# Where layer 1 of the second-to-last batches stands at the end of a two-layer graph network kernel

## The chip, the cores and the metric

The kernel runs on one core of a Trainium2 chip. A core has TensorE (PE, matmuls), VectorE (DVE), ScalarE (ACT), GpSimd (POOL) and SyncE (SP), and 16 DMA engines. Each engine works through its own queue of instructions in order; a wait in a queue holds up all that stands behind it. SP, ACT and POOL also issue DMAs. The metric is the device time of one execution in microseconds, the median over several runs.

## The reference

The input x has 32 batches of 512 rows with 512 features, and there is one adjacency matrix of 512 by 512. Per batch:

```
h = relu(layernorm(x));  x = x + (adj @ h) @ W0 + b0                 # layer 0
h = relu(layernorm(x));  x = x + attention(h; adj, Wq, Wk, Wv) @ Wo + bo   # layer 1
```

In layer 1 the mask is (1 - adj) * -1e9, so each row attends to the column where its adjacency entry is largest. Where that peak is clear enough, attention is a selection of one row: row n of the result is row idx[n] of h, times Wv times Wo. The kernel tests for this at the start and then takes `single_path`, the one profiled here. Only some of the 512 rows are ever selected (at most 336 here), so layer 1 need only be computed for those and then be handed out to all rows.

## The kernel before

A batch x is held in SBUF as four chunks of 128 rows, and five such buffers rotate (`xs`). For batch b there are three products on TensorE. `aggregate(b)` makes yT from h and adj, `layer0(b)` adds yT times W0 onto x, `layer1(b)` multiplies the selected rows of h with the product of Wv and Wo (`wvo`, kept from the start). Each product is a Strassen-like scheme of seven pieces (L364); a piece is a burst of matmuls into a PSUM bank, and its result is taken by VectorE or ScalarE (`take`, L401 and L403, L411 and L414, L421). The second piece on the same bank can't start before the first has been taken.

Around layer 1 stands a way through DRAM. `put_h` (L503) writes the rows of h by an indirect DMA into the order in which they are used, `get_h` (L515) reads the used rows back, `transpose_h` (L552) transposes them on VectorE, `hT_sum` forms the sums which the seven-piece scheme needs. After `layer1`, `put_z` (L570, L575) transposes the result z and writes it to DRAM in two parts (columns of rows 0 to 6 and 6 to S, in blocks of 32). `finish` (L579) gathers z for all rows with an indirect DMA that adds onto x in SBUF, and `store` (L598) writes x to the output.

The order is written out by hand: there is no scheduler. The loop at L620 goes over b from 0 to 32 and fills 21 lists of small jobs, `todo`, by `put(batch, step, job)`. Then it emits up to three products and, between each piece and its `take`, the jobs of one step: steps 0 to 6 go with `layer0(b)`, 7 to 13 with `aggregate(b + 1)`, 14 to 20 with `layer1(b - 1)`. Where there is no product, its jobs are simply emitted in order. So regularly TensorE does: layer 0 of b, aggregate of b + 1, layer 1 of b - 1.

The end differs. The last batch, 31, takes another way through layer 1: its h is stored plainly by SP (L500), gathered for all 512 rows (`get_all`, L522, on POOL), transposed by TensorE four blocks at a time (`transpose_all`, L529, with a copy by ACT, L530), and multiplied with `wvo` row block by row block (`layer1_rows`, L541 to L544). This way has a long latency: after the last piece of layer 0 there are the norm (L284 to L294), the relu (L302), the store, the gather, the transposes. To fill TensorE meanwhile, the kernel before holds back layer 1 of batch 29 as well as that of batch 30: TensorE does aggregate(31), layer0(31), layer1(29), layer1(30), the rows of 31. For batch 29 nothing is computed in its regular place in iteration 30 (`b != B - 2`), and layer1(29) stands at steps 7 to 13 of iteration 31, layer1(30) at steps 14 to 20.

As two batches are then late together, batch 30 needs buffers of its own: its transposed h goes into `adjT` and `adjT_s`, which are no longer used, its z into the tile h0s, the transposed z into the tile hc. And both batches get their z not by an accumulating gather but by `fetch` (L588), a plain gather into `sel` and `yT`, and by `add_z` (L593) on VectorE with an output DMA (L594) of its own. The adds stand in `layer1_rows`, two behind each row block of batch 31: those of batch 29 behind rows 0 and 1, those of batch 30 behind rows 2 and 3.

Of the kernel before, what the change touches and what calls it, by code (L numbers as in the profile page):

```python
# [8 lines left out]
F32 = mybir.dt.float32  # L9
# [8 lines left out]
P = 128  # L18
# [288 lines left out]
def single_path(ctx: ExitStack, tc: tile.TileContext, x, wv, bv, wo, bo, out, kept, room):  # L307
# [15 lines left out]
    nc = tc.nc  # L323
# [157 lines left out]
    def aggregate(b):  # L481
        return product(H0[b], H0S[b], adjT, adjT_s, take_new(yT))
# [52 lines left out]
    def layer1_rows(b):  # L535
        for r in range(C):
            bank = ps_m.tile([P, D], F32, name="mm")
            for d in range(DC):
                if d == 2 and r + 1 < C:
                    transpose_all(r + 1)  # L540
                nc.tensor.matmul(bank, hs[1][:, d, r * P:(r + 1) * P], wvo[:, d, :], start=(d == 0), stop=(d == DC - 1))  # L541
# [12 lines left out]

    def hT_sum(b, i):
        if i == 0:
            HTS[b] = adjT_s[:, :, :, 0:WIDE] if b == B - 2 else work.tile([P, 4, 2, WIDE], F32, name="hTs")
        sum_b(nc, HTS[b], HT[b], i, WIDE)

    def layer1(b):  # L560
        ZT[b] = work.tile([P, DC, 32 * S], F32, name="h0s" if b == B - 2 else "zs")
        if room < 32 * S:
            nc.gpsimd.memset(ZT[b][:, :, room:32 * S], 0.0)
        return product(wvo, wvo_t, HT[b], HTS[b], take_z(ZT[b]), WIDE)

    def put_z(b, s0, s1):
        if b not in Z:
            Z[b] = dram.tile([32 * S, D], F32, name="z")
            ZR[b] = work.tile([P, S, P], F32, name="hc" if b == B - 2 else "zr")
        nc.vector.transpose(ZR[b][:, s0:s1, :].rearrange("p s (c e) -> p s c e", c=4),  # L570
                            ZT[b][:, :, 32 * s0:32 * s1].rearrange("p c (s j) -> p s c j", j=32))
        rows = Z[b].rearrange("(s j) (q f) -> q j s f", j=32, q=4)
        for q in range(4):
            eng = nc.scalar if q > 1 and (b, s0) in ((B - 3, 6), (B - 2, 0)) else nc.sync
            eng.dma_start(rows[q][:, s0:s1, :], ZR[b][32 * q:32 * q + 32, s0:s1, :])  # L575

    def finish(b):
# [3 lines left out]
                in_offset=bass.IndirectOffsetOnAxis(ap=place[:, c:c + 1], axis=0), compute_op=ALU.add)  # L581


    late_z = {B - 3: sel, B - 2: yT}

    def fetch(b):
        for c in range(C):
            nc.gpsimd.indirect_dma_start(  # L588
                out=late_z[b][:, c, :], out_offset=None, in_=Z[b],
                in_offset=bass.IndirectOffsetOnAxis(ap=place[:, c:c + 1], axis=0))  # L590

    def add_z(b, c, eng):
        nc.vector.tensor_add(X[b][:, c, :], late_z[b][:, c, :], X[b][:, c, :])  # L593
        eng.dma_start(out[b, c * P:(c + 1) * P, :], X[b][:, c, :])  # L594

    def store(b):
# [20 lines left out]
    with tc.manual_schedule():  # L617
        nc.gpsimd.affine_select(out=upper, in_=ones, compare_op=ALU.is_ge, fill=0.0, base=-1,
                                pattern=[[1, P]], channel_multiplier=-1)
        for b in range(B + 1):  # L620
            todo = [[] for _ in range(21)]

            def put(batch, step, f, *args):
                if 0 <= batch < B:
                    todo[step].append(lambda: f(batch, *args))

            put(b - 2, 15 if b == B - 1 else 1, fetch if b > B - 2 else finish)
            if b < 2:
# [10 lines left out]
            for c, step in enumerate((1, 3, 9, 12) if b == 0 else (9, 10, 11, 12) if b == B - 2 else (14, 15, 17, 19)):  # L639
# [28 lines left out]
            for i, step in enumerate((13, 13, 13, 14) if b in (0, B - 2) else (14, 15, 16, 18)):  # L668
                put(b + 1, step, yT_sum, i)
            if b < B and b != B - 2:  # L670
                put(b - 1, 20, put_z, 6, S)
            ahead = []
            put(b + 2, 8, lambda b: ahead.append(ln0(b)))
            for c, step in enumerate((9, 10, 13, 13) if b > 0 else (8, 9, 10, 11)):
                put(b + 2, step, lambda b, c: ahead[0].stats(c), c)
            put(b + 2, 14 if b > 0 else 11, lambda b: ahead[0].power())
            put(b + 2, 17 if b > 0 else 12, lambda b: ahead[0].offset())
            for c, step in enumerate((17, 18, 19, 20) if b > 0 else (12, 13, 14, 14)):
                put(b + 2, step, lambda b, c: ahead[0].relu(c), c)
            if b == 0:  # L680
                put(0, 1, lambda b: number_rows())
                for i in (2, 3):
                    put(0, 12, lambda b, i: sum_b(nc, w0_t, w0_s, i), i)
                todo[3] += todo[4] + todo[5] + todo[6]
                run(layer0_rows(0), todo[0:4])
            if b == B - 1:
                put(b, 18, lambda b: transpose_all(0))
            if b == 1:
                tables = []
                put(1, 0, lambda b: tables.append(places()))  # L690
                put(1, 16, lambda b: look_up(tables[0]))
                for i, step in enumerate((5, 5, 6, 6)):
# [270 lines left out]
```

## Time and profile before

| | us |
|---|---|
| median of 3 runs | 1085.42 (1084.32 to 1086.23) |
| profiled execution, its own time | 1083.45 |
| its span (first to last instruction) | 1081.3 |
| PE busy | 1064.6 (98%) |
| DVE busy | 902.7 (83%) |
| POOL busy | 441.9 (41%) |
| ACT busy | 362.1 (33%) |

The profile is of one execution. Its span stands 2.1 us below the time of that execution, which takes in what lies around the instructions. In a timeline, each row has the start and the length in us, the engine, the line, the operation, its output and inputs by the program's names, and in brackets how long the engine had stood idle before and who released it. In the windows by time, the columns are the stretch, its length, the busy time of PE, of its weight loads, of DVE, ACT and POOL (with the number of instructions), the granted clock of TensorE as a share of full speed, the busy share of the DMA engines, and GB/s.

### The profile page before, as it was taken

The numbers are of one execution on the slowest core, as the hardware profiler recorded it, in microseconds if no ns is written. First come the engines' busy times: TensorE is split into PE (matmuls) and PEld (weight loads), VectorE is DVE, ScalarE is ACT, GpSimd is POOL, SyncE is SP. The second block draws the span as 40 slices with busy tenths as digits, with TensorE's granted clock in tenths as the row PEclk, the third lists the DMA queues.
The fourth block names the chain that finished last, engine by engine and source line by source line (L and its number), as shares of the span: only waits on it lengthen the run. The fifth ranks groups of instructions, "written<-read, shape, count | busy, mean of one in ns | idle before, by whom it ended". The sixth has DMA issues, their size and how long they took to land.

```text
span 1081.3 us, 15886 instructions
## 1 busy us (share of the span) xinstructions
PE 1064.6 (98%) x5404; PEld 939.3 (87%) x5404; DVE 902.7 (83%) x1850; ACT 362.1 (33%) x664; POOL 441.9 (41%) x522
## 2 busy tenths in 40 slices
PE   8999999999999999999999999999999999999996
PEld 4488998999998899988998998999998999999883
DVE  6789888888888788988888888888888888888874
ACT  6223422324432323432323432323432333442221
POOL 2024554343454343454433454433355434345513
PEclk9999999999999999999999999999999999999999
DMA  9144767666776566767656776666767666776537
GB/s 330 40 88 150 188 178 170 162 164 188 197 193 179 128 171 182 202 167 200 143 149 188 200 190 179 146 165 174 202 183 183 159 154 175 194 186 168 134 103 263
DMA packets 162443, 186.90 MB, mean 173 GB/s; under 512 B 15024, under 2 KB 102320, under 8 KB 162352
## 3 DMA queue, kind: packets, MB, share of 16 engines
q1 hardware_dynamic: 132464, 116.73, 36.4%
q0 software_dynamic: 27968, 66.61, 27.4%
q10 hardware_dynamic: 1920, 2.46, 0.7%
q8 instruction: 44, 0.72, 0.3%
q14 instruction: 47, 0.39, 0.1%
HBM read 96.28 MB, written 89.46 MB: 172 GB/s over the span
## 4 chain that ended last, share of the span: by engine, by line
PE 92%; DVE 3%; DMA 1%; POOL 1%; issue 1%; ACT 1%; SPq 0%; ACTq 0%; DVEq 0%; POOLq 0%
PE mm L364 87%; PE mm L134 1%; PE mm L206 1%; PE mm L491 1%; PE mm L541 1%; DVE st L284 1%; DMA yT<-z,place 1%; POOL x L579 1%; PE pt L106 0%; DVE x L421 0%; DMA x<-in_L_gnn_Wv_dram 0%; DVE x L471 0%; DMA hc<-hs 0%; ACT h L302 0%; DMA z<-zr 0%
## 5 line engine op out<-in xcount | busy, mean ns | idle before, releaser
L579 POOL DMA_INDIRECT x<-z,place x116 | 182.8, 1576 | 352.5 <-issue 196.7
L403 ACT COPY yT<-mm 128x512 f32<-128x512 f32 x124 | 71.9, 580 | 541.7 <-PE mm L364 482.7
L421 DVE TENSOR_TENSOR x<-mm,x 128x512 f32<-128x512 f32 x217 | 149.6, 690 | 85.7 <-PE mm L364 85.7
L302 ACT ACTIVATE h<-x,off,rstd 128x512 f32<-128x512 f32 x256 | 194.7, 807 | 54.2 <-DVE off L294 53.4
L291 POOL TENSOR_TENSOR rstd<-ve,mhalf 128x2 f32<-128x2 f32 (+1 forms) x97 | 106.7, 1100 | 229.6 <-DVE ve L290 229.0
L284 DVE BATCH_NORM_STATS2 st<-x 128x6 f32<-128x512 f32 x256 | 171.5, 670 | 2.6 <-DMA x<-in_x_dram 1.4
L364 PE MATMUL mm<-adjT_s,h0s 128*128 128x256 f32 x744 | 171.0, 379 | 0.3 <-ACT yT L403 0.3
L364 PE MATMUL mm<-w_t,sel 128*128 128x256 f32 x744 | 170.7, 379 | 0.0
L364 PEld LDWEIGHTS mm<-adjT_s,h0s 128*128 128x128 f32 x744 | 141.1, 190 | 20.4 <-ACT yT L403 1.3
L364 PEld LDWEIGHTS mm<-w_t,sel 128*128 128x128 f32 x744 | 141.3, 190 | 19.3
L503 POOL DMA_INDIRECT hs<-h,dest x124 | 128.6, 1037 | 23.8 <-issue 22.4
L364 PE MATMUL mm<-w_s,yT 128*128 128x256 f32 x496 | 117.2, 379 | 0.0
L364 PE MATMUL mm<-adjT,h 128*128 128x256 f32 x496 | 117.2, 379 | 0.0
L364 PE MATMUL mm<-hTs,wvo_t 128*128 128x168 f32 x720 | 112.5, 306 | 0.8 <-ACT zs L414 0.8
L414 ACT ACTIVATE zs<-mm,cvo_c 128x168 f32<-128x168 f32 x240 | 83.1, 398 | 77.3 <-PE mm L364 73.4
L364 PEld LDWEIGHTS mm<-hTs,wvo_t 128*128 128x128 f32 x720 | 105.4, 190 | 1.0 <-ACT zs L414 1.0
L364 PEld LDWEIGHTS mm<-adjT,h 128*128 128x128 f32 x496 | 94.2, 190 | 13.2 <-issue 0.5
L364 PEld LDWEIGHTS mm<-w_s,yT 128*128 128x128 f32 x496 | 92.9, 190 | 11.3
L471 DVE TENSOR_TENSOR x<-x,b_r 128x512 f32<-128x512 f32 x124 | 83.8, 676 | 0.0
L364 PE MATMUL mm<-hT,wvo 128*128 128x168 f32 x480 | 78.2, 306 | 0.0
L364 PEld LDWEIGHTS mm<-hT,wvo 128*128 128x128 f32 x480 | 72.7, 190 | 1.6
L401 DVE TENSOR_TENSOR yT<-mm,yT 128x512 f32<-128x512 f32 x93 | 64.0, 688 | 5.5 <-PE mm L364 1.5
(156 smaller groups left out, 1277.3 us busy)
## 6 DMA issues: line engine op xcount, KB each, us to landing
out_dram<-x SPq DMA_DIRECT2D x124, 256.0 KB
x<-in_x_dram SPq DMA_DIRECT2D x120, 256.0 KB
hc<-hs SPq DMA_DIRECT2D x124, 176.0 KB
z<-zr SPq DMA_DIRECT2D x120, 96.0 KB
z<-zr SPq DMA_DIRECT2D x118, 80.0 KB
hs<-h,dest POOLq DMA_INDIRECT x124
x<-z,place POOLq DMA_INDIRECT x116
adj_s<-in_adj_dram SPq DMA_DIRECT2D x2, 512.0 KB
```

The costliest lines, as they stand in the source:

```text
L134: nc.tensor.matmul(ps, wvT[:, j, i * P:(i + 1) * P], wo_s[:, j, :], start=(j == 0), stop=(j == DC - 1))
L284: self.nc.vector.bn_stats(st, self.src[:, self.chunks[i], :])
L291: self.nc.gpsimd.tensor_tensor(self.rstd, ve, self.mhalf[:, 0:n], ALU.pow)
L302: self.nc.scalar.activation(dst, src, AF.Relu, bias=self.off[:, i:i + 1], scale=self.rstd[:, i:i + 1])
L364: nc.tensor.matmul(bank[:, m, 0:half], lhs[:, k, m * P:(m + 1) * P], rhs[:, k, :], start=(first and m == 0 and k == 0), stop=(k == 1), ski ...
L401: nc.vector.tensor_add(dst, bank, dst)
L403: nc.scalar.copy(dst, bank)
L414: nc.scalar.activation(dst[:, m, :], bank[:, m, :], AF.Identity, bias=cvo_c[:, 2 * i + m:2 * i + m + 1])
L421: nc.vector.tensor_add(dst, bank, dst)
L471: nc.vector.tensor_add(X[b][:, c, :], X[b][:, c, :], b0_r)
L503: stored = nc.gpsimd.indirect_dma_start(out=HS[b], out_offset=bass.IndirectOffsetOnAxis(ap=dest[:, i:i + 1], axis=0), in_=H1[b][:, i, :], ...
L579: nc.gpsimd.indirect_dma_start(out=X[b][:, c, :], out_offset=None, in_=Z[b], in_offset=bass.IndirectOffsetOnAxis(ap=place[:, c:c + 1], axi ...
```

## The change

Layer 1 of batch 29 goes back to steps 14 to 20 of iteration 30. In iteration 31, steps 7 to 13 hold layer1(30), and steps 14 to 20 have no product; their jobs follow one another. TensorE then does aggregate(31), layer1(29), layer0(31), layer1(30), the rows of 31.

With it: batch 29 is finished by the accumulating gather (`finish`, at step 1 of iteration 31) and written by `store` (SP, at step 12 of iteration 31, behind the two stores of h at steps 9 and 11). Batch 30 alone is fetched late, into `yT`, and its four adds stand behind rows 2 and 3. The borrowed buffers of batch 30 are dropped. The transposes of batch 30's h move from steps 10 to 12 of iteration 31 to its steps 1 to 3, its sums from steps 12 to 14 to steps 4 and 5; z of batch 30 is put at step 13 of iteration 31 and at the start of the last iteration. In iteration 30, the sums of yT and the adds of b0 have their regular steps again.

```diff
-            for i in range(2):
-                add_z(B - 3 + r // 2, 2 * (r % 2) + i, nc.sync if r < 2 else nc.scalar)
+            if r > 1:
+                for i in range(2):
+                    add_z(B - 2, 2 * (r - 2) + i, nc.scalar)
...
-            HT[b] = adjT[:, :, 0:32 * S] if b == B - 2 else work.tile([P, DC, 32 * S], F32, name="hT")
+            HT[b] = work.tile([P, DC, 32 * S], F32, name="hT")
...
-        ZT[b] = work.tile([P, DC, 32 * S], F32, name="h0s" if b == B - 2 else "zs")
+        ZT[b] = work.tile([P, DC, 32 * S], F32, name="zs")
...
-            eng = nc.scalar if q > 1 and (b, s0) in ((B - 3, 6), (B - 2, 0)) else nc.sync
+            eng = nc.scalar if q > 1 and (b, s0) == (B - 2, 0) else nc.sync
...
-            put(b - 2, 15 if b == B - 1 else 1, fetch if b > B - 2 else finish)
+            put(b - 2, 1, fetch if b == B else finish)
...
-            put(b - 2, 14 if b == B - 1 else 0, put_z, 0, 6)
-            if b == B - 1:
-                put(b - 2, 13, put_z, 6, S)
-            for r, step in enumerate((10, 11, 12) if b in (1, B - 1) else (5, 7, 8) if b < B else ()):
+            put(b - 2, 0, put_z, 0, 6)
+            for r, step in enumerate((10, 11, 12) if b == 1 else (1, 2, 3) if b == B - 1 else (5, 7, 8) if b < B else ()):
                 put(b - 1, step, transpose_h, r)
...
-            if b < B - 1:
+            if b < B:
                 put(b - 2, 12, store)
...
-            for i, step in enumerate((12, 13, 13, 14) if b in (1, B - 1) else (11, 11, 12, 12) if b < B else ()):
+            for i, step in enumerate((12, 13, 13, 14) if b == 1 else (4, 4, 5, 5) if b == B - 1 else (11, 11, 12, 12) if b < B else ()):
                 put(b - 1, step, hT_sum, i)
...
-            if b < B and b != B - 2:
-                put(b - 1, 20, put_z, 6, S)
+            if b < B:
+                put(b - 1, 13 if b == B - 1 else 20, put_z, 6, S)
...
-            run(aggregate(b + 1) if b + 1 < B else layer1(b - 2) if b < B else None, todo[7:14])
-            run(layer1(b - 1) if 0 < b < B and b != B - 2 else None, todo[14:21])
+            run(aggregate(b + 1) if b + 1 < B else layer1(b - 1) if b < B else None, todo[7:14])
+            run(layer1(b - 1) if 0 < b < B - 1 else None, todo[14:21])
```

More of the change, by code (lines that the diff above doesn't have):

```diff
@@ L556, in hT_sum @@
         if i == 0:
-            HTS[b] = adjT_s[:, :, :, 0:WIDE] if b == B - 2 else work.tile([P, 4, 2, WIDE], F32, name="hTs")
+            HTS[b] = work.tile([P, 4, 2, WIDE], F32, name="hTs")
         sum_b(nc, HTS[b], HT[b], i, WIDE)
     def layer1(b):
-        ZT[b] = work.tile([P, DC, 32 * S], F32, name="h0s" if b == B - 2 else "zs")
+        ZT[b] = work.tile([P, DC, 32 * S], F32, name="zs")
         if room < 32 * S:
@@ L568, in put_z @@
             Z[b] = dram.tile([32 * S, D], F32, name="z")
-            ZR[b] = work.tile([P, S, P], F32, name="hc" if b == B - 2 else "zr")
+            ZR[b] = work.tile([P, S, P], F32, name="zr")
         nc.vector.transpose(ZR[b][:, s0:s1, :].rearrange("p s (c e) -> p s c e", c=4),
@@ L581, in finish @@
                 in_offset=bass.IndirectOffsetOnAxis(ap=place[:, c:c + 1], axis=0), compute_op=ALU.add)
-    late_z = {B - 3: sel, B - 2: yT}
     def fetch(b):
@@ L588, in fetch @@
             nc.gpsimd.indirect_dma_start(
-                out=late_z[b][:, c, :], out_offset=None, in_=Z[b],
+                out=yT[:, c, :], out_offset=None, in_=Z[b],
                 in_offset=bass.IndirectOffsetOnAxis(ap=place[:, c:c + 1], axis=0))
     def add_z(b, c, eng):
-        nc.vector.tensor_add(X[b][:, c, :], late_z[b][:, c, :], X[b][:, c, :])
+        nc.vector.tensor_add(X[b][:, c, :], yT[:, c, :], X[b][:, c, :])
         eng.dma_start(out[b, c * P:(c + 1) * P, :], X[b][:, c, :])
@@ L633, in single_path @@
                 put(b + 1, step, h0_sum, i)
-            put(b - 2, 14 if b == B - 1 else 0, put_z, 0, 6)
-            if b == B - 1:
-                put(b - 2, 13, put_z, 6, S)
-            for r, step in enumerate((10, 11, 12) if b in (1, B - 1) else (5, 7, 8) if b < B else ()):
+            put(b - 2, 0, put_z, 0, 6)
+            for r, step in enumerate((10, 11, 12) if b == 1 else (1, 2, 3) if b == B - 1 else (5, 7, 8) if b < B else ()):
                 put(b - 1, step, transpose_h, r)
-            for c, step in enumerate((1, 3, 9, 12) if b == 0 else (9, 10, 11, 12) if b == B - 2 else (14, 15, 17, 19)):
+            for c, step in enumerate((1, 3, 9, 12) if b == 0 else (14, 15, 17, 19)):
                 put(b + 1, step, add_b0, c)
@@ L665, in single_path @@
                     put(b, 15 + c, add_cvo, c)
-            for i, step in enumerate((12, 13, 13, 14) if b in (1, B - 1) else (11, 11, 12, 12) if b < B else ()):
+            for i, step in enumerate((12, 13, 13, 14) if b == 1 else (4, 4, 5, 5) if b == B - 1 else (11, 11, 12, 12) if b < B else ()):
                 put(b - 1, step, hT_sum, i)
-            for i, step in enumerate((13, 13, 13, 14) if b in (0, B - 2) else (14, 15, 16, 18)):
+            for i, step in enumerate((13, 13, 13, 14) if b == 0 else (14, 15, 16, 18)):
                 put(b + 1, step, yT_sum, i)
-            if b < B and b != B - 2:
-                put(b - 1, 20, put_z, 6, S)
+            if b < B:
+                put(b - 1, 13 if b == B - 1 else 20, put_z, 6, S)
             ahead = []
```

## The prediction

> **What bounds the kernel now.** I read the page first: TensorE busy 98% of the span, and the chain that ended last is 92% TensorE. So an edit counts if it makes TensorE wait, or if it changes what follows TensorE's last matmul. The change touches only the last two batches, so I then read the timeline of TensorE from 985 us on.
>
> ```profile
> span 1081.3 us, 15886 instructions
> PE 1064.6 (98%) x5404; PEld 939.3 (87%) x5404; DVE 902.7 (83%) x1850; ACT 362.1 (33%) x664; POOL 441.9 (41%) x522
> ```
>
> ```profile
> 995.20 1.30 PE L364 MATMUL mm<-hT,wvo 128*128 128x168 f32 x8
> ...
> 1003.18 1.89 PE L364 MATMUL mm<-w_s,yT 128*128 128x256 f32 x8
> ...
> 1027.35 1.89 PE L364 MATMUL mm<-w_s,yT 128*128 128x256 f32 x8
> ...
> 1039.44 1.30 PE L364 MATMUL mm<-hT,wvo 128*128 128x168 f32 x8
> ...
> 1044.94 1.41 PE L364 MATMUL mm<-hTs,wvo_t 128*128 128x168 f32 x8 [0.78 <-ACT zs L414]
> ...
> 1048.46 1.30 PE L364 MATMUL mm<-adjT,wvo 128*128 128x168 f32 x8
> ...
> 1055.06 0.60 PE L529 MATMUL pt<-ident,h 128*128 128x128 f32 x4
> ...
> 1057.78 1.88 PE L541 MATMUL mm<-wvo,h 128*128 128x512 f32 x4
> ...
> 1067.68 5.32 PE L541 MATMUL mm<-wvo,h 128*128 128x512 f32 x12
> ```
>
> Layer 1 in its regular slot takes 995.20 to 1003.18 = 7.98 us without a gap. Layer 0 of batch 31 runs 1027.35 to 1039.44 (12.09), layer 1 of batch 29 to 1048.46 (9.02, two small stalls in it), layer 1 of batch 30 with the first transposes to 1057.78, the four row blocks of batch 31 to 1073.00. All of TensorE's waits here together are about 1.4 us. What runs beside it is the last batch's own way: norm, relu, store of h, indirect gather, transposes. From the timelines of SyncE, GpSimd and VectorE:
>
> ```profile
> 1044.33 2.37 SPq L500 DMA_DIRECT2D hs<-h  x2
> 1049.82 1.18 POOL L522 DMA_INDIRECT h<-hs,idx  x1 [5.88 <-PE mm L364]
> 1059.95 0.97 POOL L588 DMA_INDIRECT sel<-z,place  x1 [4.80 <-PE pt L529]
> 1064.33 0.69 DVE L593 TENSOR_TENSOR x<-sel,x 128x512 f32<-128x512 f32 x1 [1.79 <-DMA sel<-z,place]
> ```
>
> The wait of the gather of h is put down to a matmul that had long ended; the trace's semaphore marks show the second store of h landing at 1049.01, and that is what it waited for. The end of the chain of waits shows that the tail is not TensorE's:
>
> ```profile
> 1067.84 1.73 PE mm L541 x4
> 1069.58 0.21 issue
> 1069.78 6.57 DMA yT<-z,place
> 1076.35 0.02 issue
> 1076.38 0.69 DVE x L593
> ```
>
> The last matmul ends at 1073.00 and the span at 1081.33: a tail of 8.33 us, set by the eighth late gather of z (6.57 us in loaded DMA engines).
>
> [...] the last matmul ends at 1073.0, and the windows by time show the clock at half from about 1076.4, 3.4 us later.
>
> ```profile
> 1075.00:1076.00 1.00, 0.00 (x0) 0.00 (x0) 0.75 (x2) 0.00 (x0) 0.00 (x0) 1.00 0.96 358
> 1076.00:1077.00 1.00, 0.00 (x0) 0.00 (x0) 0.62 (x1) 0.00 (x0) 0.00 (x0) 0.70 1.00 371
> 1077.00:1078.00 1.00, 0.00 (x0) 0.00 (x0) 0.07 (x1) 0.00 (x0) 0.00 (x0) 0.50 0.76 277
> ```
>
> [...]
>
> **The change part by part.**
>
> *TensorE order.* Layer 1 of batch 29 moves ahead of layer 0 of batch 31, at its regular 7.98 us. The instructions stay the same. Layer 0 of batch 31 then starts at 1027.35 + 7.98 = 1035.33 and ends at 1047.42. Layer 1 of batch 30 follows and takes 9.02 us, as that of batch 29 did in the same place behind layer 0 with the same ScalarE order (its 0.78 us stall stays): 1056.44.
>
> *The last batch's way.* It hangs on the end of layer 0. Second store of h issued at 1046.3, 6.9 us after 1039.44; gather begun at 1049.82, 10.38 us after; so now 1054.3 and 1057.80. The first gather of h landed 3.57 us after its start (semaphore marks 1053.39); the first late gather of z was 4.38 us from start to the add. I take 3.57: 1061.4. The range is 3.1 (1.9 to the first packet, 0.8 of data, 0.4) to 4.4. TensorE thus **stands still from 1056.44 to 1061.4, 5.0 us**, where before it had layer 1 of batch 30 to do.
>
> *First transposes bare.* Before, the copy of the first transposes hid behind two pieces of layer 1. Now it is exposed: transposes at 1055.06, copy until 1056.29, weight load and matmul: 1.35 us. Rows begin at 1062.75, and with 1073.00 - 1057.78 = 15.22 us end at 1077.97. Later rows of h land at most 5.5 us after the start of their own gathers and each is needed 3.87 us after the one before, so they do not stop it. TensorE ends **4.97 us later**.
>
> *The tail.* Four late gathers, adds and stores go (batch 29 returns to the accumulating gather, L579, and to stores from SyncE). The last row add begins 0.2 us after the last matmul; two adds of batch 30 follow at 0.61 us each; the last ends 2.1 us after the matmul. Three stores of 256 KB then land: 0.9 us to the first packet, 1.97 us for 768 KB at some 390 GB/s, 0.35 to the semaphore, about 4.15 us after the matmul; from the last landing (1080.30) to the end were 1.03 us. That is 5.2; with some straggling 5.4 instead of 8.33: **2.9 us won**.
>
> *The clock.* [...] Weighted 0.5 us.
>
> *Moved at no cost, with its cover.* The norm sums, transposes and sums of batch 30's hT on VectorE go into layer 0 of batch 31: three transposes (0.71, 0.69, 0.57) and four sums of 0.5, 4 us, beside its seven adds of 0.69 and one transpose of zr 0.97; 9.8 of 12.09 us, and where the adds waited for matmuls (1.03 us each) they did so with room for two sums. Uncovered, up to 1 us of stall. The accumulating gathers of batch 29 (four of 1.57 us on GpSimd) run 6.6 us into layer 0, as at 1009.80 before, and end at about 1049.2, when the first rstd is due; VectorE needs that only after a statistic, so 0 to 0.1 us. SyncE's four stores of batch 29 stand right behind h: 1 MB, 2.6 us, finished at about 1059.3, before the gather's first packet (1059.7); uncovered, up to 2.6 us on the landing of h. Then z of batch 30: two of its stores stand on ScalarE behind the exposed copy of the first transposes, so go out at 1062.6 to 1063.4 and land at about 1066.6 (3.2 us from issue before); four gathers from 1067.4 on, landing until at most 1077.8 with the 6.57 us of before. Their adds are due at 1074.7 to 1079.3: hidden, with 1.5 us to spare.
>
> *Sum.* + 4.97 - 2.9 + 0.5 = + 2.6 us. Span 1083.9, and the profiled execution 1083.45 would be 1086.05. The median of runs is 1085.42, 1.97 us above the profiled execution; I carry that over: **1088.0 us**.
>
> **The rivals.** A difference within 0.2% (2.17 us) is what a measurement of this kernel cannot tell from none.
>
> *Small loss, within the band (27%).* The clock holds, the first gather lands after 3.1 us since the small packets of z no longer run beside it, and the three last stores land without straggling: 4.5 - 3.1 = 1.4 us, 1086.8. For it: the DMA engines stand nearly idle from 1033 to 1045 before. Against: 1 MB of stores is put exactly there.
>
> *Large loss (13%).* The stores of batch 29 do hold up h: 1 to 2.6 us on the landing or the gather, the idle stretch becomes 6 to 7.5 us[...]: 2.05 + 1.8 + 1.4 = 5.2 us, 1090.7. [...]
>
> *Faster (5%).* The place is the tail. If batch 30's adds are all done early, only the last row's own add and store stand behind the matmul: 0.2 + 0.69 + 0.05 + 0.9 + 0.7 + 0.35 + 1.03 = 3.9 us, 4.4 won. To be faster by 2.17 us the rows must end by 1075.26, and the transposes begin by 1058.7, within a microsecond of the gather's start. No gather in this trace comes near that. At 1058.7 the time would be 1083.2.
>
> That the change does not do what it says is excluded: the built order of instructions has layer 1 of batch 29 ahead of layer 0.
>
> **How the numbers follow.** The likeliest case, a loss of 2.2 to 4 us with or without the half clock, has 55%. With the rivals: slower 0.68, within 0.2% 0.27, faster 0.05. Its own range is 1087.6 to 1089.4; the 8-in-10 range leaves out the faster case and the lower end of the small loss (0.1) and the worst of the large loss (under 0.1): 1086.3 to 1090.8.
>
> **What would show it.** In the profile after: no gap between aggregate of batch 31, layer 1 of batch 29 and layer 0; a TensorE gap of about 5 us before L529, with the wait on the gather of h; the rows starting near 1062.7; the clock dipping inside or after that gap in some executions; a tail of 5 to 6 us that ends in out stores, not in a gather. I am wrong if layer 0 of batch 31 has new stalls on VectorE, if the gather of h starts more than 10.4 us after layer 0, or if the tail still waits for z.

## The result and the profile after

| | before | after |
|---|---|---|
| median | 1084.87 us (1083.42 to 1086.23, 4 runs) | 1091.37 us (1091.15 to 1092.18, 4 runs) |
| profiled execution, its own time | 1083.45 | 1091.38 |
| its span | 1081.3 | 1089.7 |

The ratio of after to before is 1.0064 [1.0052, 1.0076]: slower by 6.5 us. The forecast was 1088.0 us with a range up to 1090.8. So the direction was right, and the loss is more than twice the 2.6 us of the sum. The sum is compared below with the two profiled executions, whose spans are 8.4 us apart. That of before was one of its faster ones, 1.4 us under its median.

The page of after, first its span and then the busy time of the engines:

```profile
span 1089.7 us, 15886 instructions
PE 1067.2 (98%) x5404; PEld 940.3 (86%) x5404; DVE 899.7 (83%) x1846; ACT 362.3 (33%) x664; POOL 446.8 (41%) x522
```

The instructions are as many as before, and TensorE is even 2.6 us longer busy with the same 5404 matmuls. It ran slower somewhere. The timeline of TensorE of after, from layer 1 of batch 29 on, says where:

```profile
1028.21 1.30 PE L364 MATMUL mm<-hT,wvo 128*128 128x168 f32 x8
...
1036.19 1.89 PE L364 MATMUL mm<-w_s,yT 128*128 128x256 f32 x8
...
1048.28 1.30 PE L364 MATMUL mm<-hT,wvo 128*128 128x168 f32 x8
...
1056.20 1.30 PE L364 MATMUL mm<-hTs,wvo 128*128 128x168 f32 x8
1064.08 1.12 PE L529 MATMUL pt<-ident,h 128*128 128x128 f32 x4 [6.58 <-DMA h<-hs,idx]
1065.87 3.78 PE L541 MATMUL mm<-wvo,h 128*128 128x512 f32 x4 [0.67 <-ACT h L530]
...
1077.73 5.32 PE L541 MATMUL mm<-wvo,h 128*128 128x512 f32 x12
```

Layer 1 of batch 29 takes 7.98 us, layer 0 of batch 31 12.09, both as forecast and without a gap; layer 1 of batch 30 takes 9.2 to 1057.50, where the idle time begins. Then TensorE stands still for 6.58 us, not 5.0, waiting for the gather of h. When it goes on, four transposes take 1.12 us (0.60 before) and the first row block 3.78 us for four matmuls (1.88 before). From the first row block to the end of the rows it is 17.2 us, 1065.87 to 1083.05, where before it was 15.2.

The windows by time of after (stretch, length, busy time of PE, its loads, DVE, ACT, POOL, clock, DMA share, GB/s) show the cause of the slow matmuls:

```profile
1061.00:1062.00 1.00, 0.00 (x0) 0.00 (x0) 0.12 (x1) 0.00 (x0) 0.69 (x2) 1.00 1.03 188
1062.00:1063.00 1.00, 0.00 (x0) 0.00 (x0) 0.00 (x0) 0.00 (x0) 0.70 (x2) 0.91 0.54 119
1063.00:1064.00 1.00, 0.00 (x0) 0.00 (x0) 0.00 (x0) 0.00 (x0) 0.69 (x2) 0.50 0.89 291
...
1068.00:1069.00 1.00, 1.00 (x2) 0.30 (x2) 0.00 (x0) 0.00 (x0) 0.00 (x0) 0.50 0.30 88
1069.00:1070.00 1.00, 1.00 (x6) 0.56 (x5) 0.00 (x0) 0.00 (x0) 0.00 (x0) 0.68 0.00 0
1070.00:1071.00 1.00, 1.00 (x5) 0.52 (x4) 0.00 (x0) 0.59 (x1) 0.96 (x1) 1.00 0.00 0
```

The clock falls at 1062.8, while TensorE stands still, and is back only at 1069.6, by the trace's clock records. That is 6.8 us, and the last 5.6 us of it lie behind the start of the transposes. Such a loss was in the forecast, but as 0.5 us, which was the author's estimate.

The chain that ended last, from the second store of h to the last add (start, length, what):

```profile
1055.18 3.64 DMA hs<-h
...
1059.61 4.42 DMA h<-hs,idx
...
1083.69 1.28 DVE x L592 x2
```

Its two transfers are both longer than before. The second store of h is issued 6.9 us after layer 0 ends (1048.28 to 1055.18), just as before. But it took 2.70 us to land before, by the semaphore marks, and takes 3.64 here. The gather of h took 3.57, and takes 4.42. These are 0.94 and 0.85 us, together 1.8: the 1.6 us by which the idle stretch outgrew its forecast, and 0.2 by which layer 1 of batch 30 ahead of it ended later (9.2 us for 9.02; most of this is the end of its last matmuls, which the forecast's count leaves out: counted like it, it took 9.06). What stands beside these transfers is shown by the timelines of SyncE and GpSimd of after:

```profile
1053.20 2.37 SPq L500 DMA_DIRECT2D hs<-h  x2
1055.99 2.35 SPq L597 DMA_DIRECT2D out_dram<-x  x4
1058.43 3.50 SPq L576 DMA_DIRECT2D z<-zr  x6
1059.61 1.52 POOL L522 DMA_INDIRECT h<-hs,idx  x1 [6.76 <-DMA hs<-h]
1061.44 0.99 POOL L522 DMA_INDIRECT h<-hs,idx  x1 [0.31 <-issue]
```

The four stores of batch 29 (1 MB) stand right behind h, as the forecast feared in its large loss. The first gather also keeps GpSimd busy for 1.52 us; before it was 1.18.

**Where the 8.4 us of span went.** 0.86 of it lies ahead of the change (layer 0 of batch 31 ends at 1048.28, not 1039.44 + 7.98 = 1047.42). Then: the forecast loss of cover and bare transposes 4.97, the later store and gather 1.8, transposes and rows at half clock 0.44 + 1.97 = 2.4. The end of the rows thus comes 9.2 us later than that of before against the same mark. The tail, from there to the end of the span, is 6.6 us and not 8.3, which gives 1.7 back. 9.2 - 1.7 = 7.5, and with the 0.86 it is 8.4.

### The profile page after: what moved, and what is told of

Same layout as the page of the kernel before. It is cut to its first block, busy times and chain, and to the rows that moved or that the text cites. A ratio compares the mean times of both kernels' runs of the same rounds, so it can differ in the third digit from the quotient of the medians.

```text
span 1089.7 us, 15886 instructions
## 1 busy us (share of the span) xinstructions
PE 1067.2 (98%) x5404; PEld 940.3 (86%) x5404; DVE 899.7 (83%) x1846; ACT 362.3 (33%) x664; POOL 446.8 (41%) x522
## 4 chain that ended last, share of the span: by engine, by line
PE 87%; DVE 4%; DMA 3%; POOL 2%; issue 1%; ACT 1%; SPq 1%; POOLq 0%; DVEq 0%; ACTq 0%
PE mm L364 81%; POOL x L580 2%; PE mm L541 1%; PE mm L206 1%; PE mm L491 1%; PE mm L134 1%; DMA z<-zr 1%; DMA x<-in_L_gnn_Wo_dram 1%; ACT h L302 1%; DVE st L284 1%; DMA hs<-h,dest 1%; DVE zr L571 0%; DVE x L421 0%; DMA h<-hs,idx 0%; DVE zs L411 0%
## 5 line engine op out<-in xcount | busy, mean ns | idle before, releaser
L580 POOL DMA_INDIRECT x<-z,place x120 | 189.2, 1576 | 369.4 <-issue 197.3
L503 POOL DMA_INDIRECT hs<-h,dest x124 | 131.6, 1062 | 23.8 <-issue 22.6
L364 PE MATMUL mm<-hTs,wvo_t 128*128 128x168 f32 x744 | 116.3, 306 | 0.8 <-ACT zs L414 0.8
L414 ACT ACTIVATE zs<-mm,cvo_c 128x168 f32<-128x168 f32 x248 | 85.9, 397 | 81.1 <-PE mm L364 81.1
L364 PEld LDWEIGHTS mm<-hTs,wvo_t 128*128 128x128 f32 x744 | 108.9, 190 | 1.1 <-ACT zs L414 1.1
L364 PE MATMUL mm<-hT,wvo 128*128 128x168 f32 x496 | 80.8, 306 | 0.0
L364 PEld LDWEIGHTS mm<-hT,wvo 128*128 128x128 f32 x496 | 75.1, 190 | 1.6
```

Of the source, the lines that this page charges most:

```text
L364: nc.tensor.matmul(bank[:, m, 0:half], lhs[:, k, m * P:(m + 1) * P], rhs[:, k, :], start=(first and m == 0 and k == 0), stop=(k == 1), ski ...
L414: nc.scalar.activation(dst[:, m, :], bank[:, m, :], AF.Identity, bias=cvo_c[:, 2 * i + m:2 * i + m + 1])
L503: stored = nc.gpsimd.indirect_dma_start(out=HS[b], out_offset=bass.IndirectOffsetOnAxis(ap=dest[:, i:i + 1], axis=0), in_=H1[b][:, i, :], ...
L580: nc.gpsimd.indirect_dma_start(out=X[b][:, c, :], out_offset=None, in_=Z[b], in_offset=bass.IndirectOffsetOnAxis(ap=place[:, c:c + 1], axi ...
```

## The experiments

The questions were: what makes the store and the gather of h longer, what does the clock cost, what keeps the tail at 6.6 us, and is anything else left. All kernels are after with one edit or some of them, but for the last, which is before with one edit. They all compute the whole result. Four theories are about the way of h. Two are about its landing. A: the stores of batch 29 that stand behind h on SyncE hold it up (the large loss of the forecast). F: loads of instructions, which the DMA view lists as a queue of their own, fall on it. Two are about the gather: V, VectorE at work makes the issue on GpSimd longer (1.52 us, in before 1.18); Z, other transfers beside the gather slow it.

The table sums them up. "h lands" and "gather" are the two transfers in the chain of waits (last store of h, first gather of h), "rows" is from the first row block to the end of the last. "Loss" compares profiled spans: from the end of layer 0 of batch 31 to the end of the span, less the same of before without layer 1 of batch 29 (1081.3 - 1039.44 - 7.98 = 33.9), so that what lies ahead of the change drops out. Times are in us; a ratio is to before on the same chip.

| kernel | time | ratio | h lands | gather | rows | loss |
|---|---|---|---|---|---|---|
| after | 1091.37 | 1.0064 [1.0052, 1.0076] | 3.64 | 4.42 | 17.2 | 7.5 |
| e1 stores later | 1091.89 | 1.0065 [1.0042, 1.0089] | 3.63 | 4.34 | 17.9 | 8.0 |
| e2 TensorE kept busy | 1088.79 | 1.0032 [1.0020, 1.0043] | 3.65 | 4.18 | 15.3 | 5.1 |
| e3 both, less busy | 1090.64 | 1.0053 [1.0036, 1.0070] | 3.63 | 4.36 | 15.3 | 4.8 |
| e4 stores after z | 1091.92 | 1.0066 [1.0050, 1.0083] | 3.62 | 5.01 | 17.5 | 8.1 |
| e5 SyncE, GpSimd shifted | 1091.54 | 1.0066 [1.0049, 1.0083] | 3.65 | 4.36 | 16.8 | 6.8 |
| e6 VectorE quiet | 1091.90 | 1.0063 [1.0046, 1.0080] | 3.64 | 4.28 | 17.6 | 7.8 |
| e7 early adds | 1091.46 | 1.0061 [1.0044, 1.0078] | 3.63 | 4.53 | 17.1 | 6.6 |
| e8 e2 + e5 + e6 + e7 | 1089.82 | 1.0047 [1.0030, 1.0063] | 3.64 | 4.09 | 15.9 | 4.6 |
| e9 all queues shifted | 1091.62 | 1.0058 [1.0039, 1.0078] | 2.74 | 4.44 | 17.6 | 6.8 |
| e10 gather alone | 1094.36 | one run | 3.62 | 3.48 | 17.5 | 7.6 |
| e11 e8 + e9 | 1089.15 | 1.0039 [1.0022, 1.0056] | 2.73 | 4.24 | 16.3 | 4.3 |

**e1, the stores of batch 29 moved away from h.** They are issued behind the first row block.

```diff
+            if r == 0:
+                store(B - 3)
...
-            if b < B:
+            if b < B - 1:
                 put(b - 2, 12, store)
```

> The changed kernel with the four stores of batch 29 moved from right behind the two stores of h to behind row block 0 of batch 31. Theory A, these stores hold up the way of h: from the issue of the second store of h to the start of its gather 3.5 us as before (4.4 in the changed kernel), first gather 3.6 us to landing (4.4), so TensorE's idle stretch falls from 6.6 to some 4.8 us and the time by 1.8 us or, where the clock no longer drops, by up to 4.2: 1087.2 to 1089.6. Theory B, the landing is slow for a reason of its own (straggling DMA engines, the accumulating gather of batch 29): idle stretch stays at 6.6, time 1091.4.

The timelines of SyncE and GpSimd, and the row of TensorE behind its idle stretch, of e1:

```profile
1054.33 2.37 SPq L500 DMA_DIRECT2D hs<-h  x2
1059.00 4.05 SPq L578 DMA_DIRECT2D z<-zr  x6
1060.73 1.53 POOL L522 DMA_INDIRECT h<-hs,idx  x1 [6.76 <-DMA hs<-h]
1065.12 1.12 PE L529 MATMUL pt<-ident,h 128*128 128x128 f32 x4 [6.50 <-DMA h<-hs,idx]
```

Nothing is issued on SyncE for 2.3 us behind h now, and yet GpSimd waits the same 6.76 us, the store lands after the same 3.63 us, and TensorE idles 6.50 us for 6.58. Theory A falls, and with it the large loss of the forecast, whose time came nearest: the megabyte behind h on SyncE didn't hold up its landing (3.64 us with it, 3.63 without).

**e4, the same stores put behind the first of z.** Both stay near the gather; what follows h directly on SyncE is now z.

```diff
-            if b < B:
+            if b < B - 1:
                 put(b - 2, 12, store)
...
+            if b == B - 1:
+                put(b - 2, 14, store)
```

> The changed kernel with the four stores of batch 29 behind the first four stores of z of batch 30 on SyncE: out of the way of the landing of h, but now beside its gather. Theory A1, the delay of the landing (0.9 us) comes from stores behind h[...]: landing to gather start again 3.5 us after the second issue. Theory A2, the delay of the gather (0.85 us) comes from stores beside it: the first gather still 4.4 us or more. Time by A1 alone 0.9 lower, 1090.5; if the stores now press on the gather harder, 1091.4 or above.

The landing of h stays at 3.62 us, so it isn't the kind of transfer behind it that counts. The gather became longer, 5.01 us from 1059.33 on: SyncE now issues the megabyte of batch 29 from 1059.51 to 1061.40, in the midst of it. That is a first sign for Z.

**e2, TensorE kept busy in the idle stretch.** Seven matmuls on constants are put behind layer 1 of batch 30; nothing reads their result.

```diff
+    def keep_busy(n):
+        bank = ps_m.tile([P, D], F32, name="mm")
+        for i in range(n):
+            nc.tensor.matmul(bank, ident, wvo[:, i % DC, :], start=(i == 0), stop=(i == n - 1))
...
+                put(b, 18, lambda b: keep_busy(7))
```

> The changed kernel with seven matmuls of 128x512 on constants (about 6.0 us, result never read) in TensorE's idle stretch ahead of the first transposes. Theory A, the half clock costs 2.4 us (0.44 in the first transposes and their way to the rows, 1.97 in the rows): rows again 15.2 us long, time 2.4 us lower, 1089.0. Theory B, the rows are long for want of data and not for the clock: no change, 1091.4, or more where the seven matmuls end after the landing.

The timeline of TensorE of e2 (L529 holds the added matmuls, each of which is two in the trace):

```profile
1057.95 6.17 PE L529 MATMUL mm<-wvo,ident 128*128 128x512 f32 x14
1064.78 0.66 PE L534 MATMUL pt<-ident,h 128*128 128x128 f32 x4 [0.66 <-DMA h<-hs,idx]
1066.11 1.98 PE L546 MATMUL mm<-wvo,h 128*128 128x512 f32 x4 [0.68 <-issue]
...
1076.11 5.32 PE L546 MATMUL mm<-wvo,h 128*128 128x512 f32 x12
```

The transposes are back at 0.66 us and the rows at 15.3. The gather still ends late, but the clock holds: 1088.79 us, and the interval of its ratio lies below that of after. So the half clock is shown to cost a good part of the 6.5 us: 2.6 by the medians, 3.5 by the ratios. The kernel stays slower than before by 3.4 us all the same: still no useful work fills the stretch.

**e3, e1 and five such matmuls.** Its diff is the two above with `keep_busy(5)`.

> Both edits: stores of batch 29 behind row block 0, and five such matmuls (4.3 us) in the then shorter idle stretch. If the two causes are separate and add up: 1.8 + 2.4 = 4.2 us less than the changed kernel, 1087.2, some 2.3 us above the kernel before, which is the bare price of the lost cover less the shorter tail. If one was only the other in disguise: no better than the better of the two alone.

In the profiled execution TensorE idles 2.23 us behind the matmuls, and the clock stayed up (0.999 over the span, rows 15.3). In its other executions the mean clock was 0.996 to 0.997. That doesn't show that it fell in this stretch: the mean takes in the whole execution, and before, which has no such stretch, has means of 0.996 to 0.999. In the profiles of e10 and e12 the clock is at half for 3.4 us near 102 us, over 900 us ahead of the change. The time of 1090.64 us lies between after and e2, and its interval overlaps both. So how much has to be filled for the clock to hold is left open.

**e5, the instruction loads moved.** If F is right, the late landing hangs on which instruction of SyncE's or GpSimd's stream is fetched when, and a few more instructions far ahead must move it. Behind each of the four stores of h of batch 28, GpSimd gets three more memsets of a small tile, and the output stores of two earlier batches are split into halves on SyncE.

```diff
-            nc.gpsimd.memset(gap, 0.0)
+            for _ in range(4 if b == B - 4 else 1):
+                nc.gpsimd.memset(gap, 0.0)
...
+        parts = 2 if b in (B - 6, B - 5) else 1
...
+            for h in range(parts):
+                p0, p1 = h * P // parts, (h + 1) * P // parts
+                nc.sync.dma_start(out[b, c * P + p0:c * P + p1, :], X[b][p0:p1, c, :])
```

> The changed kernel with eight more DMAs on SyncE (two earlier outputs stored in halves) and twelve more small memsets on GpSimd, both two iterations earlier, so that both queues reach their next block of instructions before h is stored. Theory F: two loads of 8 KB of instructions, which begin 1.9 and 2.5 us after the issue of the second store of h in the changed kernel and in all four experiments so far, [...]: then the second store lands 2.7 us after its issue, the gather begins 0.9 us earlier, and the time is 0.9 us lower, 1090.5. Theory A (stores or other data) or a slow pair of DMA engines: landing still 3.6 us after the issue, time 1091.4.

**e9, the streams of VectorE and ScalarE shifted as well.** To e5 it adds twelve copies of one column on each of the two, in iteration 29.

```diff
+    spare = [num.tile([P, 1], F32, name=f"spare{i}") for i in range(2)]
...
+            if b == B - 3:
+                for i in range(12):
+                    put(b, 2 + i, lambda b: nc.scalar.copy(spare[0], ones[:, 0:1]))
+                    put(b, 2 + i, lambda b: nc.vector.tensor_copy(spare[1], ones[:, 0:1]))
```

> The shifts of e5 and, two iterations before the end, twelve tiny copies more each on ScalarE and VectorE. In e5 one of the two loads of instructions went away from the stores of h and with it one of the two late landing marks (3.06 us); the load that begins 1.9 us after the second issue stayed, and the mark at 3.64 us with it. Theory F: that load belongs to ScalarE's or VectorE's queue; now it goes too, all sixteen marks of the second store come by 2.7 us, the gather begins 0.9 us earlier than in the changed kernel, time 0.9 lower, 1090.5. If the mark at 3.64 us stays without the load, theory F falls.

The DMA view of after, 1055 to 1059 us, lists two queues: SyncE's, and one for instructions.

```profile
q1 hardware_dynamic: 685, 1.28, 84.6%
q14 instruction: 2, 0.02, 1.0%
```

The same view of e5, 1054.8 to 1058.8:

```profile
q1 hardware_dynamic: 698, 1.30, 85.8%
q14 instruction: 1, 0.01, 0.5%
```

And of e9, 1054 to 1058, with no instruction queue left, and then its chain of waits:

```profile
q1 hardware_dynamic: 705, 1.35, 86.9%
```

```profile
1054.93 2.74 DMA hs<-h
...
1058.47 4.44 DMA h<-hs,idx
```

The trace has 16 marks of the second store of h on its semaphore, and GpSimd, which waits for it, goes on 0.02 us behind the last one: at 1049.03 in before (mark at 1049.01), at 1058.84 in after (1058.82). Sorted, the marks end with (us after the issue):

| | loads of 8 KB of instructions begin | the last four marks |
|---|---|---|
| before | none near | 2.68, 2.68, 2.69, 2.70 |
| after | 1.88 and 2.47 | 2.69, 2.71, 3.06, 3.64 |
| e5 | 1.88 | 2.70, 2.71, 2.72, 3.65 |
| e9 | none near | 2.69, 2.70, 2.73, 2.74 |

With one load gone, one late mark is gone; with both gone, both are. In after, 14 of 16 were there at 2.71 us, and GpSimd went on behind the last, at 3.64. The other profiles agree: after, e1 to e4, e6, e7 and e10 have two such loads and two late marks each, e5 and e8 one of each, before, e9, e11 and e12 none. So F is shown for the landing: 0.93 us of the loss in the profile are two loads of instructions that the edit's shift of the program happened to put on the landing of h. In e9 the gather begins 3.54 us after the second store of h, as in before (3.51), where after has 4.43. The time didn't follow: 1091.62. The transposes of e9 begin 0.75 us earlier after layer 0 than in after, but TensorE still idles 5.71 us, the clock falls, and its rows take 17.6 us, 0.4 more than in after.

**e6, VectorE quiet during the gather.** Three of the four adds of `cvo`, which stood in the idle stretch, move into `layer1_rows`.

```diff
+            if r + 1 < C:
+                add_cvo(b, r + 1)
...
-                for c in range(C):
-                    put(b, 15 + c, add_cvo, c)
+                put(b, 15, add_cvo, 0)
```

> The changed kernel with three of the four adds of cvo on batch 31 moved from VectorE's queue before the gather of h to between the row blocks[...]. Theory V: [...] then 1.0 to 1.2 us, landing 0.3 to 0.5 us earlier, time 1091.0. Otherwise the first gather still takes 1.5 us to issue and 4.4 to land, time 1091.4.

**e10, the gather alone.** To e6 it adds that the stores of batch 29 (as in e1) and those of z of batch 30, now all on ScalarE, come after the gather of h.

```diff
+            if b == B:
+                put(b - 2, 0, put_z, 6, S)
...
-            eng = nc.scalar if q > 1 and (b, s0) == (B - 2, 0) else nc.sync
+            eng = nc.scalar if b == B - 2 else nc.sync
...
-            if b < B:
-                put(b - 1, 13 if b == B - 1 else 20, put_z, 6, S)
+            if b < B - 1:
+                put(b - 1, 20, put_z, 6, S)
```

> The changed kernel with the stores of batch 29 behind row block 0, all eight stores of z of batch 30 behind the first transposes (on ScalarE), and the adds of cvo between the row blocks: nothing else is in the DMA engines while h is gathered. Theory Z: the 4.4 us of the first gather (3.6 before) come from small packets of z beside it: then [...] landing 3.1 to 3.4 us after the start. Otherwise it stays near the 4.3 us of e6. Its time says little, since z comes late.

The gather of e6 on GpSimd, and in the chain of waits:

```profile
1060.38 1.03 POOL L522 DMA_INDIRECT h<-hs,idx  x1 [6.76 <-DMA hs<-h]
...
1060.38 4.28 DMA h<-hs,idx
```

And of e10:

```profile
1062.45 1.03 POOL L522 DMA_INDIRECT h<-hs,idx  x1 [6.75 <-DMA hs<-h]
...
1062.45 3.48 DMA h<-hs,idx
```

With VectorE quiet, GpSimd is done with the gather in 1.03 us, not 1.52. Work on VectorE alone is not enough for the longer time: in e9 adds of `cvo` lie beside the whole of the first gather's issue, in e12 a transpose and adds do. The rows are of e9 and of e12:

```profile
1058.47 1.21 POOL L524 DMA_INDIRECT h<-hs,idx  x1 [5.87 <-DMA hs<-h]
...
1053.58 1.03 POOL L522 DMA_INDIRECT h<-hs,idx  x1 [5.92 <-PE mm L364]
```

So V holds in this place: without the work that stood beside the issue in after, it is 0.5 us shorter; which kind of work makes it longer, and how, is not shown. And of the 0.5 us only 0.1 reached the landing (4.28). Without other transfers beside it the gather takes 3.48 us, 0.8 less than in e6, which supports Z, by one profile. But Z doesn't explain why the gather was longer in after than in before. The DMA views of the first gather of h show what the other queues carried meanwhile: in before (1049.82 to 1053.39) two of them, and in e1 (1060.73 to 1065.07) one.

```profile
q1 hardware_dynamic: 401, 0.19, 20.5%
q10 hardware_dynamic: 352, 0.16, 15.7%
...
q1 hardware_dynamic: 766, 0.36, 29.8%
```

That is 0.35 MB in before and 0.36 MB in e1, yet the gather took 3.57 us in the one and 4.34 in the other. The longer issue is 0.35 us of this at most (1.53 for 1.18); the rest stays open. In e10 nothing is won in time: z of batch 30 is late now, the idle stretch of 5.62 us still costs the clock, and one run took 1094.36 us, of which 2.9 lie ahead of the change (layer 0 of batch 31 ends at 1051.13).

**e7, the adds of z a row block earlier.** They stand behind row blocks 1 and 2, so that only the last row's own add and store come after the last matmul.

```diff
-            if r > 1:
+            if r in (1, 2):
                 for i in range(2):
-                    add_z(B - 2, 2 * (r - 2) + i, nc.scalar)
+                    add_z(B - 2, 2 * (r - 1) + i, nc.scalar)
```

> The changed kernel with the late adds of batch 30 behind row blocks 1 and 2 instead of 2 and 3. If the tail is set by VectorE's two adds and ScalarE's last store behind the last row block, it falls by two adds of 0.61 us, from 6.6 to some 5.4 us, time 1090.2; if ScalarE's last instructions and the loading of its code for the jump at the end set it, by up to 1.5 us, 1089.9. If the fetch of z is not there in time, the row blocks' adds wait and nothing is won.

The end of the chain of waits of e7 is now the row's own add:

```profile
1079.16 5.17 PE mm L541 x12
...
1084.35 0.69 DVE x L543
```

From the last matmul at 1084.32 to the end of the span it is 5.7 us, where after has 6.6. So the place was right, with 0.9 us in the profile; in the time it doesn't show (1091.46). Executions of one kernel differ by about as much ahead of the change: in this profile layer 0 of batch 31 ended 1.26 us later than in that of after.

**e8, and e11: everything together.** e8 has e5, e6, e7 and six matmuls as in e2. e11 has e8, the shift of e9 and one more short matmul, of 256 columns, behind the transposes.

```diff
+                put(b, 18, lambda b: keep_busy(6))
...
+                put(b, 18, lambda b: keep_busy(1, 256))
```

> All of it in the changed kernel: six matmuls on constants in the idle stretch (5.2 us), shifted instruction blocks, the adds of cvo between the row blocks, the late adds behind row blocks 1 and 2. If the terms are separate: 1091.4 - 2.4 - 0.9 - 0.4 - 1.3 = 1086.4 us, 1 us above the kernel before: what is left is the cover that layer 1 of batch 29 gave, 5 us, less the shorter tail. If one of the theories F and V is wrong, 1087 to 1088.

> All of e8 (matmuls on constants, adds of cvo between the row blocks, late adds behind row blocks 1 and 2) with the shifts of e9, and a short matmul behind the first transposes. If the terms add up: landing of h 0.9 us earlier than in e8, time 1089.8 - 0.9 = 1088.9, and where the clock now stays up in every execution (e8 had it lower in three of four) up to 1.5 us less, 1087.4: still 2 to 3.5 us above the kernel before, which would be what the lost cover costs by itself less what the tail gives.

The timeline of TensorE of e11:

```profile
1058.18 5.31 PE L531 MATMUL mm<-wvo,ident 128*128 128x512 f32 x12
1063.84 0.66 PE L536 MATMUL pt<-ident,h 128*128 128x128 f32 x4 [0.35 <-DMA h<-hs,idx]
...
1077.77 3.70 PE L548 MATMUL mm<-wvo,h 128*128 128x512 f32 x8 [0.71 <-ACT h L537]
```

Clock, landing of h and tail are all mended in e11, and the loss in the profile goes from 7.5 us to 4.3; 0.71 of what is left is a wait that the edit itself made (the last row block waits for ScalarE, on which the early stores of z now stand ahead of its copy). In time, 1089.15 and 1089.82 us are below after, but not below e2, and e8 is 3.4 us above the 1086.4 to which its terms had been added up. What e5 to e9 add to e2 is seen in the profiles only and is not shown in the time.

**e12, the kernel before with its two small stalls smoothed.** In before, layer 1 of batch 29 and of batch 30 stall 0.78 and 0.64 us for ScalarE, whose relu of batch 31 is in the way. One relu and the first store of h move from step 9 to step 10 for that batch, and z of batch 29 goes out on SyncE alone.

```diff
-            eng = nc.scalar if q > 1 and (b, s0) in ((B - 3, 6), (B - 2, 0)) else nc.sync
+            eng = nc.scalar if q > 1 and (b, s0) == (B - 2, 0) else nc.sync
...
-            put(b, 9 if b > 0 else 7, lambda b: halves[0].relu(1, b < B - 1))
-            put(b, 9, put_h, 0)
+            put(b, 10 if b == B - 1 else 9 if b > 0 else 7, lambda b: halves[0].relu(1, b < B - 1))
+            put(b, 10 if b == B - 1 else 9, put_h, 0)
```

> The kernel before, with the second relu of the last batch behind the third eviction of layer 1 of batch 29 instead of ahead of it, and all stores of z of batch 29 on SyncE instead of two on ScalarE. If TensorE's two stalls there (0.78 and 0.64 us) are paid in full, because the last fetch of z hangs on the end of layer 1 of batch 30: both stalls gone, the end 1.0 to 1.4 us earlier, 1083.7 to 1084.1 against some 1085.0, and so faster than both kernels. If the tail is set by the loaded DMA engines alone, or z of batch 29 now comes later and delays the fetches: no change or up to 1 us more.

The timeline of TensorE of e12, and then the end of its chain of waits:

```profile
1047.97 1.41 PE L364 MATMUL mm<-hTs,wvo_t 128*128 128x168 f32 x8
...
1057.56 0.66 PE L529 MATMUL pt<-ident,h 128*128 128x128 f32 x4 [0.20 <-DMA h<-hs,idx]
```

```profile
1072.71 7.36 DMA yT<-z,place
...
1080.09 0.69 DVE x L593
```

Both stalls are gone; a wait of 0.20 us for the gather of h is new. From the end of layer 0 to the end of the rows it is 32.4 us (1043.15 to 1075.55) instead of 33.6. But the tail doesn't hang on TensorE: the last gather of z takes 7.36 us instead of 6.57, and the tail is 9.4 us instead of 8.3, so 1.1 of the 1.2 us are given back. Over 21 runs of e12 and 25 of before the medians are 1084.88 and 1085.84 us, the ratio is 0.9993 [0.9985, 1.0001]: not clear of no change. No version tried is shown to beat before.

## Why the prediction was wrong in size

- **Order and the moved work: right.** Layer 1 of batch 29 in its slot (7.98 us), layer 0 (12.09), layer 1 of batch 30 (9.06 for 9.02, counted to the end of its issue) came as worked out. VectorE's and GpSimd's moved jobs made no gap in any of them: up to 1 us had been put down in case of no cover.
- **The lost cover: right.** 4.97 us was the term for the idle stretch and the bare transposes, and it stands as the largest one of the account: without the later store and gather (1.8) and the half clock (2.4), 5.0 of the 9.2 us are left. No run changes this term alone.
- **Failed: "so now 1054.3 and 1057.80", the way from layer 0 to the gather taken over as 10.38 us.** It was 11.33 (1048.28 to 1059.61). The store was issued on time, but the landing had two loads of instructions on it, 0.93 us; e5 took one of them away, e9 both, and only with both gone the 0.93 us went. The prediction treated a latency that had been measured once as one of the store, without asking what else used the DMA engines in that moment. Its own mark for being wrong, "if the gather of h starts more than 10.4 us after layer 0", is what happened.
- **Failed: "I take 3.57".** The gather took 4.42 us, at the upper end that was named (4.4). The small loss had even taken it for 3.1, an estimate: in before, the first packet of its queue is at 1051.72, 1.9 us after its start; the 0.8 us for the data and the 0.4 behind them were the author's. Alone it takes 3.48 (e10), so traffic beside it can cost 0.8 us, and the shorter issue (e6) gives 0.1. But before had traffic beside it too; what made the 0.85 us between before and after stays open.
- **Failed: "Weighted 0.5 us" for the clock.** It measured 2.4. The weight was the author's estimate: before shows the clock fall once, 3.4 us behind the last matmul (1073.0 to 1076.4), and nothing in it says how often an idle stretch of 5.0 us brings that. With 6.58 us idle the clock fell, as it did in all eight profiles whose stretch was 5.6 us or longer (after, e1, e4 to e7, e9, e10). And it stayed at half for 6.8 us, from 1062.8 to 1069.6, though TensorE was at work again from 1064.08 on.
- **Failed: the tail, "with some straggling 5.4".** It was 6.6, so 1.7 us won and not 2.9. The last store lands 4.8 us after the last matmul (1087.88; 4.15 was forecast), and the end comes 1.8 us behind that, not 1.03. The terms of the 4.15 agree with what before shows: from the issue of the first store of h to its first packet 0.9 us (1044.33 to 1045.23), 388 GB/s from 1073.00 to 1076.40, from the last packet of the second store of h to its landing 0.36 us (1048.65 to 1049.01). The 1.8 us are the exit of ScalarE, told below.
- **The median.** The sum of the forecast was 2.6 us, and its own terms measured 4.97 + 1.8 + 2.4 - 1.7 = 7.5: short by 4.9. That the time ended only 3.4 us above the forecast comes from the 1.97 us added for the distance of the profiled execution to the median, which wasn't there (the profile of after lies at its median); 0.86 us ahead of the change and 0.4 less between span and time make up the rest. The number came closer than the sum by luck.
- **The rivals.** The large loss, 1090.7 us, came nearest in time, by an idle stretch of the length that it named (6 to 7.5) and 1.4 us for the clock in its sum. Its cause, the stores of batch 29, is refuted by e1 and e4. The gain of the tail exists (e7), but a microsecond of it can't outweigh the lost cover: with clock, loads and tail mended (e11) there remains a loss of 4.3 us in the profile.

## What to carry to other kernels

When work that covers a latency is taken away, the bare latency isn't the whole price: where TensorE's gap came to 5.6 us and more here, the half clock behind it cost another 2.0 to 3.1 us (0.44 in the first transposes, and what the rows take above 15.2). A transfer's time from one profile is one of that moment; where it becomes bare, look at all other transfers of that moment, instruction loads among them, and give it a range of a microsecond. And before a stall is removed, see whether the end waits for TensorE or for a transfer behind it.

## What was not expected of the hardware

- **Instruction loads delayed a store's landing.** With two loads of 8 KB on it, a store of 512 KB counted as landed at 3.64 us instead of 2.70: with each load, one of its 16 marks was late (3.06 and 3.64, the others by 2.71). A few small instructions more on each engine, two iterations and more ahead, moved them away (e9).
- **From the last issue of ScalarE or SyncE to the end of the span it took 3.9 to 4.6 us.** In after, ScalarE's last store is issued by 1085.34 us and its branch out of the program begins at 1085.37; its next instruction starts at 1088.76, 3.4 us later, and the span ends 0.9 us after that. In before it was 1077.47 to 1080.41, 2.9 us. SyncE had seen the last store land at 1087.96, so in after all waited for ScalarE: the end came 4.3 us behind that engine's last issue (3.9 in before). In e7 ScalarE starts again at 1086.63, 2.1 us earlier, and the last store has landed by 1087.67, but SyncE is then the last: its last store is issued by 1085.40, its next instruction starts at 1088.36, and the end comes at 1090.01, 4.6 us behind that issue. Loads of instructions lie in these stretches; whether the way out waits for one was not tried.
- **How long half clock lasted.** Where the clock came back in these traces, it had been down for 3.4 us near 102 us in e10 and e12, and around the start of the rows for 6.8 us in after, e5, e7, e9 and e10 and for 10.2 us in e1, e4 and e6. In after, TensorE had been at work again for 5.6 us of it, but for 0.67 us before the rows. Nor did the fall come at one distance from the end of TensorE's work: it was 3.4 us in before (1073.0 to 1076.4), 5.3 in after (1057.50 to 1062.82) and 2.7 in e6 (1058.26 to 1060.92). Two rows of e6's windows by time, from its clock's steps, show the stretch ahead of that fall, with 0.76 us of work, and one at half clock with 2.36:

```profile
1057.50:1060.92 3.42, 0.76 (x6) 0.50 (x4) 2.54 (x4) 0.69 (x2) 0.54 (x1) 1.00 1.03 380
...
1064.33:1067.74 3.41, 2.36 (x6) 1.45 (x7) 0.00 (x0) 0.58 (x1) 0.89 (x1) 0.50 0.88 257
```

What sets these times is not shown by the traces.
